# Fetching adjacency blocks in pairs, and the steps behind them one block later

## The chip, the cores and the metric

The kernel runs on one core of a Trainium2 chip. The metric is the device time of one launch in microseconds; the time shown for the kernel before is the median of three runs. The profile is of one execution, and its span runs from the first to the last instruction.

## The reference

One layer of graph attention over 4096 rows with 4 heads, then a residual and a layer norm:

```python
ht = (h @ W).reshape(N, 4, 512).transpose(1, 0, 2)
src = einsum('hnd,hd->hn', ht, a[:, :512, 0]); dst = einsum('hnd,hd->hn', ht, a[:, 512:, 0])
e = leaky_relu(src[:, :, None] + dst[:, None, :], 0.01) + adj_mat[None]
att = softmax(e, axis=-1)
h_prime = einsum('hij,hjd->hid', att, ht)
x = layernorm(x + h_prime.mean(axis=0))
```

x is 4096 x 512, adj 4096 x 4096, W 512 x 2048, a 4 x 1024 x 1, all float32. The entries of adj go up to 1e9, while the scores beside them are small. So in nearly every row of the softmax one column has all the weight: the column of the row's largest entry of adj, when it leads the second largest by enough. Then h_prime of that row is x of that column times the mean of W over heads.

## The kernel before

`leading_rows` computes every row on that assumption and counts the rows for which it can't be shown to hold (`test`, `count`, `report`); `general` computes blocks with such rows in full and runs only if there are any. With these inputs there are none, and `general` isn't entered.

The 4096 rows are cut into 32 blocks of 128, one row per partition. Row p*32 + ib belongs to block ib, so in DRAM a partition's rows of two neighbouring blocks lie side by side (adj_rows, line 99). A block of adj is 128 x 4096 float32, 2.1 MB. For each block ib:

- `segment_maxima` (VectorE, line 180, two instructions): the maximum of each segment of 16, 32 or 64 columns of adj.
- `find_segment` (lines 187 and 189, VectorE): the largest segment maximum and which segment holds it. `fetch_segment` (GpSimd, lines 196 to 207): an indirect DMA gathers that segment of each row again from DRAM, the tile lead.
- `find_column` (VectorE, lines 217 and 223, then GpSimd, lines 225 and 211): the place inside the segment, the column, and an indirect DMA that gathers the row of x for each column, the tile y.
- `turn` (PE, line 238, with a copy on ScalarE, line 240), `residual` (line 246, adds x) and `products` (line 253, y by w_sum) into one PSUM tile.
- `stats` (ScalarE, lines 275 and 277), `row_norm` (line 260), `rstd` (GpSimd, lines 280 to 282) and `finish` (line 286) make the layer norm, into the tile hold. Stores from hold are issued after the loop.

The schedule is written by hand: every engine runs its instructions in program order. The loop over t has step 1 of block t, and behind it `find_column` of block t - 2, which stands between the two halves of the reduction of block t, `turn`, `residual` and `products` of block t - 3, `stats` of block t - 4 and, every second t, `finish` of two blocks from t - 6. Through t = 14 the loop also turns and multiplies W by a on PE (`turn_w`, `head_vector`).

SP issues all plain loads and stores in order. adj has a ring of six buffers (adj_pool, AHEAD + 1); block t + 5 is issued at t, into the buffer of block t - 1, once that has been reduced. Blocks 28 to 30 are loaded in two parts and block 31 in four. x is loaded straight into hold by `load_x`: blocks 0 to 3 before the loop, 4 to 11 at t = 3, 12 to 15 at t = 11, 16 to 23 at t = 15, 28 to 31 at t = 26 and the rest at t = 31. W comes first, into the part of hold that later rows of x take. ScalarE issues the loads of a, GpSimd the gathers.

Of the kernel before, what the change touches and what calls it, by code (L numbers as in the profile page):

```python
# [9 lines left out]
F32 = mybir.dt.float32  # L10
# [60 lines left out]
def leading_rows(ctx, tc, x, adj, W, a, out, ident, v, n_bad, any_bad):  # L71
# [14 lines left out]
    PIECES = 4  # L86
    LATE = NB - Q
    BEHIND = LATE - Q

    once = ctx.enter_context(tc.tile_pool(name="once", bufs=1))  # L90
    adj_pool = ctx.enter_context(tc.tile_pool(name="adj_pool", bufs=AHEAD + 1))
    y_pool = ctx.enter_context(tc.tile_pool(name="y_pool", bufs=4))
    lead_pool = ctx.enter_context(tc.tile_pool(name="lead_pool", bufs=1))
    LEADS = (8, 8, LAST)
# [3 lines left out]

    adj_rows = adj.rearrange("(p nb) m -> nb p m", nb=NB)
    spans = ((E_EARLY, 0, EARLY), (E, EARLY, NB - LAST), (E_LAST, NB - LAST, NB))  # L100
    adj_segs = {e: adj.rearrange("n (s e) -> (n s) e", e=e) for e, _, _ in spans}
    x_rows = x.rearrange("(p nb) d -> p nb d", nb=NB)
    out_rows = out.rearrange("(p nb) d -> p nb d", nb=NB)
# [1 line left out]


    once.tile([P, 24], F32, name="pad")
    hold = once.tile([P, NB, D], F32, name="hold")
    w_at = NB - KB * H
    w_sum = once.tile([P, KB, D], F32, name="w_sum")  # L110
# [5 lines left out]
    def pieces(ib):  # L116
        return PIECES if ib == NB - 1 else 2 if ib >= LATE else 1

    def load_adj(ib):
        if 0 <= ib < NB:  # L120
            t = adj_t[ib] = adj_pool.tile([P, N], F32, name="adj_t")
            n = pieces(ib)
            for k in range(n):
                nc.sync.dma_start(t[:, ts(k, N // n)], adj_rows[ib][:, ts(k, N // n)])  # L124

    def load_x(lo, n):
        nc.sync.dma_start(hold[:, ds(lo, n), :], x_rows[:, ds(lo, n), :])
# [3 lines left out]

    load_adj(0)
    for s in range(2):
        for h in range(0, H, H // 2):
            nc.scalar.dma_start(
                a_rows[ds(s * H + h, H // 2), :], a[ds(h, H // 2), ts(s, D), :].rearrange("h d o -> h (d o)")
            )
    for kb in range(0, KB, 2):
        load_w(kb, 2)
        load_adj(kb // 2 + 1)  # L140
    for ib in range(KB // 2 + 1, AHEAD):
        load_adj(ib)
    load_x(0, Q)

    make_identity(nc, ident)
# [73 lines left out]
    def find_column(ib):  # L219
        if ib < BEHIND:  # L220
            find_inner(ib)
        within = small.tile([P, 8], U32, name="within")
        nc.vector.max_index(within, top[:, ib, :], lead_of[ib])  # L223
        col = small.tile([P, 1], U32, name="col")
        nc.gpsimd.tensor_tensor(col, at_of.pop(ib), within[:, 0:1], op=OP.add)  # L225
        gather_rows(ib, col)
# [31 lines left out]
    def row_norm(ib):  # L258
        sq = rows.tile([P, D], F32, name="sq")
        nc.scalar.activation(sq, hold[:, ib, :], AF.Square, accum_out=xx[:, ib : ib + 1])  # L260

    def put_by(ib):

        if ib == BEHIND:
            o_ps["by"] = adj_pool.tile([P, N // D, D], F32, name="adj_t")
        nc.scalar.copy(o_ps["by"][:, ib - BEHIND, :], o_ps.pop(ib))

    def add_x(engine, ib):
# [159 lines left out]
    vectors = [(kb, h) for kb in range(KB) for h in range(H)]  # L428
    vectors_at = {t: 2 if t < 3 else 1 for t in range(1, 15)}
    COLUMN, PROJECT, STATS, FINISH = 2, 3, 4, 6  # L430

    for t in range(NB):
        if t == NB // 2:
            tc.mark_branch_hint_location("general", engines=HINTED)
        if t in x_at:
            load_x(*x_at[t])
        if t + AHEAD == NB - 1:
            load_x(LATE, Q)
        load_adj(t + AHEAD)
        middle = 1 if t == NB - 1 else 2  # L440
        segment_maxima(t, 0, middle)
        if t >= COLUMN:
            find_column(t - COLUMN)
        segment_maxima(t, middle, PIECES)
        pair = FINISH <= t < BEHIND + FINISH and t % 2 == 0
        if pair:
            rstd(slice(t - FINISH, t - FINISH + 2))
        if t == NB - 1:
            for ib in (BEHIND, BEHIND + 2):
                load_x(ib, 2)  # L450
        find_segment(t)
        if t < 2:
            mean_of_heads(t)
        elif t == 2:
            mean_of_heads(2)
            mean_of_heads(3)
        if t == 0:
            turn_a()
        turned = [(*vectors[0], turn_w(*vectors.pop(0))) for _ in range(vectors_at.get(t, 0))]
        if t == 16:  # L460
            head_norms()
        ib = t - PROJECT
        if t == NB - 1:
            for late in range(LATE, NB):
                row_norm(late)
        if t == NB - 2:
            residual(LATE)
            residual(LATE + 1)
        if ib >= 0:
            turn(ib)  # L470
            if ib > BEHIND:
                products(ib - 1, KB - 1, KB)
            if ib < BEHIND:
                residual(ib)
        for some in turned:
            head_vector(*some)
        if ib >= 0:
            products(ib, 0, KB if ib < BEHIND else KB - 1)
        if t >= BEHIND + STATS:
            put_by(t - STATS)  # L480
        elif t >= STATS:
            stats(t - STATS)
            row_norm(t - STATS)
        if pair:
            finish(t - FINISH)
            finish(t - FINISH + 1)

    for ib in range(BEHIND, LATE):
        row_norm(ib)
# [217 lines left out]
```

## Time and profile before

| | |
|---|---|
| median of three runs | 235.0 us (234.98 to 235.17) |
| profiled execution | 234.9 us |
| its span | 233.4 us |
| busy: PE, VectorE, ScalarE, GpSimd | 199.9, 191.3, 111.8, 100.7 us |
| moved by DMA | 97.12 MB, of it 88.54 read from HBM and 8.39 written |
| mean DMA rate over the span | 416 GB/s |
| granted PE clock | 0.965 |

"Idle before" of an instruction is the time for which its engine had nothing to run ahead of it, and the releaser is what ended it. PE's busy time is modelled and says little on how full it is. A DMA's time to landing runs from its issue and so holds the time in which it stands behind others. In the slices each digit is a fortieth of the span in tenths.

### The profile page before, as it was taken

To read this page: it belongs to the slowest core of one execution; us is meant where nothing else is said; L and a number is where in the kernel's file an instruction comes from. 1 tells how busy PE (TensorE), PEld (TensorE's weight loads), DVE (VectorE), ACT (ScalarE), POOL (GpSimd) and SP (SyncE) were. 2 spreads that over 40 slices of the span, in tenths; PEclk is the share of its full clock that TensorE was granted. 3 is DMA by queue.
4 is the path that set the end of the run, shared out by engine and by line. 5 is a ranking of instruction groups with operands and counts; after the bars stand their busy time and mean duration, and the time that the engine had idled before them with its cause. 6 is when DMAs were issued, how large, how long until landed. Compare 5 with 4: busy or idle time off the path is not lost.

```text
span 233.4 us, 2484 instructions
## 1 busy us (share of the span) xinstructions
PE 199.9 (86%) x683; PEld 105.3 (45%) x683; DVE 191.3 (82%) x300; ACT 111.8 (48%) x267; POOL 100.7 (43%) x215
## 2 busy tenths in 40 slices
PE   0069995999999999999999779879998977999980
PEld 0034644646565555665645244334443433444460
DVE  0548299689929999999788995999999999998881
ACT  2001223014474757575767455545664644188561
POOL 2020234414524464644543452647464564548300
PEclk9999999579999999999999979999999999999997
DMA  6999999999999999999999999999999999999995
GB/s 237 423 432 428 428 438 426 415 439 436 422 421 437 423 431 425 431 419 428 430 430 428 432 423 432 423 430 421 426 433 420 426 423 426 412 424 420 421 414 213
DMA packets 12257, 97.12 MB, mean 416 GB/s; under 512 B 1992, under 2 KB 2440, under 8 KB 6480
## 3 DMA queue, kind: packets, MB, share of 16 engines
q1 hardware_dynamic: 8640, 88.08, 89.1%
q0 software_dynamic: 3584, 8.84, 9.6%
q8 instruction: 6, 0.10, 0.2%
q14 instruction: 11, 0.09, 0.1%
q10 hardware_dynamic: 16, 0.02, 0.0%
HBM read 88.54 MB, written 8.39 MB: 415 GB/s over the span
## 4 chain that ended last, share of the span: by engine, by line
DMA 64%; DVE 21%; PE 11%; SPq 1%; issue 1%; ACT 0%; DVEq 0%
DMA adj_t<-in_adj_dram 53%; DVE seg L180 17%; DMA hold<-in_x_dram 11%; PE o L253 6%; PE o L295 2%; DVE at L189 1%; PE tp L238 1%; DVE top L187 1%; PE o L246 1%; DVE within L223 1%; SPq L130 1%; PE o L291 0%; SPq L124 0%; DVE inner L217 0%; ACT hold L335 0%
## 5 line engine op out<-in xcount | busy, mean ns | idle before, releaser
L180 DVE TENSOR_REDUCE seg<-adj_t 128x128 f32<-128x2048 f32 (+3 forms) x66 | 145.5, 2208 | 28.5 <-DMA adj_t<-in_adj_dram 28.2
L253 PE MATMUL o<-w_sum,yt 128*128 128x512 f32 x248 | 117.6, 616 | 0.7 <-ACT yt L240 0.7
L253 PEld LDWEIGHTS o<-w_sum,yt 128*128 128x128 f32 x248 | 45.6, 196 | 55.2 <-issue 43.9
L240 ACT COPY yt<-tp 128x512 f32<-128x512 f32 x32 | 18.8, 588 | 43.9 <-PE tp L238 43.8
L200 POOL DMA_INDIRECT lead<-in_adj_dram,row x32 | 32.3, 1008 | 14.6 <-POOL row L196 14.6
L211 POOL DMA_INDIRECT y<-in_x_dram,col x32 | 30.9, 964 | 15.4 <-POOL col L225 15.1
L238 PE MATMUL tp<-ident,y 128*128 128x128 f32 x128 | 22.1, 296 | 10.2 <-DMA y<-in_x_dram,col 10.1
L246 PE MATMUL o<-hold,ident 128*128 128x512 f32 x52 | 28.5, 634 | 1.7 <-DMA hold<-in_x_dram 1.7
L343 PE MATMUL o<-hold,ident 128*128 128x512 f32 x32 | 17.3, 696 | 13.6 <-DMA hold<-in_L_gnn_W_dram 13.6
L238 PEld LDWEIGHTS tp<-ident,y 128*128 128x128 f32 x128 | 18.5, 209 | 22.8 <-issue 20.5
L361 ACT COPY wt<-tp 128x512 f32<-128x512 f32 x16 | 9.2, 587 | 38.2 <-PE tp L359 38.2
L196 POOL TENSOR_TENSOR row<-at,first 128x1 uint32<-128x1 uint32 x32 | 6.1, 190 | 43.6 <-DVE at L189 43.6
L367 PEld LDWEIGHTS pv<-at_d,wt 128*128 128x128 f32 x128 | 17.2, 200 | 7.4 <-ACT wt L361 3.7
L260 ACT ACTIVATE sq<-hold 128x512 f32<-128x512 f32 x32 | 19.8, 620 | 0.0
L225 POOL TENSOR_TENSOR col<-start,within 128x1 uint32<-128x1 uint32 x31 | 5.9, 190 | 32.2 <-DVE within L223 32.2
L286 ACT ACTIVATE hold<-o,nm,sd 128x512 f32<-128x512 f32 x24 | 17.2, 771 | 0.0
L277 ACT ACTIVATE sq<-o,nm 128x512 f32<-128x512 f32 x24 | 16.5, 687 | 0.8
L343 PEld LDWEIGHTS o<-hold,ident 128*128 128x128 f32 x32 | 6.9, 225 | 21.5 <-issue 21.5
L367 PE MATMUL pv<-at_d,wt 128*128 128x2 f32 x128 | 16.0, 249 | 0.6 <-ACT wt L361 0.6
L344 ACT ACTIVATE w_sum<-o 128x512 f32<-128x512 f32 x4 | 2.4, 598 | 27.5 <-PE o L343 27.5
L275 ACT ACTIVATE sq<-o 128x512 f32<-128x512 f32 x24 | 14.5, 606 | 0.0
L187 DVE MAX8 top<-seg 128x8 f32<-128x256 f32 (+2 forms) x32 | 11.6, 362 | 1.1
(86 smaller groups left out, 140.0 us busy)
## 6 DMA issues: line engine op xcount, KB each, us to landing
adj_t<-in_adj_dram SPq DMA_DIRECT2D x28, 2048.0 KB, 30.8
adj_t<-in_adj_dram SPq DMA_DIRECT2D x6, 1024.0 KB, 28.1
hold<-in_L_gnn_W_dram SPq DMA_DIRECT2D x2, 2048.0 KB, 16.4
hold<-in_x_dram SPq DMA_DIRECT2D x2, 2048.0 KB, 37.6
out_dram<-hold SPq DMA_DIRECT2D x4, 1024.0 KB, 16.1
out_dram<-hold SPq DMA_DIRECT2D x7, 512.0 KB, 14.4
hold<-in_x_dram SPq DMA_DIRECT2D x3, 1024.0 KB
adj_t<-in_adj_dram SPq DMA_DIRECT2D x4, 512.0 KB, 19.8
```

The lines of the kernel that those rows point to most:

```text
L180: nc.vector.tensor_reduce(seg_of[ib][:, ts(k, N // e // n)], adj_t[ib][:, ts(k, N // n)].rearrange("p (s e) -> p s e", e=e), axis=AX.X, op ...
L200: nc.gpsimd.indirect_dma_start(out=lead, out_offset=None, in_=adj_segs[e], in_offset=bass.IndirectOffsetOnAxis(ap=row[:, :1], axis=0),)
L211: nc.gpsimd.indirect_dma_start(out=y, out_offset=None, in_=x, in_offset=bass.IndirectOffsetOnAxis(ap=col[:, :1], axis=0),)
L238: nc.tensor.transpose(tp[:, kb, :], y[:, ds(kb, P, KB)], ident)
L240: nc.scalar.copy(yt, tp)
L246: nc.tensor.matmul(o_ps[ib], ident, hold[:, ib, :], start=start, stop=False)
L253: nc.tensor.matmul(o_ps[ib], yt_of[ib][:, kb, :], w_sum[:, kb, :], start=(start and kb == 0), stop=(kb == KB - 1),)
L260: nc.scalar.activation(sq, hold[:, ib, :], AF.Square, accum_out=xx[:, ib : ib + 1])
L277: nc.scalar.activation(sq, o, AF.Square, bias=nm[:, i], accum_out=sd[:, i])
L286: nc.scalar.activation(hold[:, ib, :], o_ps.pop(ib), AF.Identity, bias=nm[:, i], scale=sd[:, i])
L343: nc.tensor.matmul(o, ident, hold[:, w_at + kb * H + h, :], start=(h == 0), stop=(h == H - 1))
L367: nc.tensor.matmul(pv[:, kb, h : 2 * H : H], wt[:, k, :], at_d[:, k, h : 2 * H : H], start=(k == 0), stop=(k == KB - 1),)
```

## The change

The pool of six adj buffers becomes one tile, ring, with six slots; block ib is in slot ib % 6. A new function `load_pair` fetches two blocks with one transfer into two neighbouring slots. The blocks named by PAIRED (4 to 15) are for the pair branch of the loop, which issues at every even t. From t = 5 to t = 18 (SLACK) what stands behind `find_segment` runs one block later than before (`steps` holds t - 1 instead of t; at t = 5 it is empty, at t = 19 it holds 18 and 19). The rows of a are loaded by two transfers instead of four. `put_by` takes the same slot of the ring as before. Reductions, index searches, gathers and products themselves are unchanged.

```diff
--- before.py
+++ after.py
@@ -86,9 +86,10 @@
     PIECES = 4
     LATE = NB - Q
     BEHIND = LATE - Q
+    SLOTS = AHEAD + 1
+    PAIRED = range(4, 16)
 
     once = ctx.enter_context(tc.tile_pool(name="once", bufs=1))
-    adj_pool = ctx.enter_context(tc.tile_pool(name="adj_pool", bufs=AHEAD + 1))
     y_pool = ctx.enter_context(tc.tile_pool(name="y_pool", bufs=4))
     lead_pool = ctx.enter_context(tc.tile_pool(name="lead_pool", bufs=1))
     LEADS = (8, 8, LAST)
@@ -98,6 +99,7 @@
 
     adj_rows = adj.rearrange("(p nb) m -> nb p m", nb=NB)
     spans = ((E_EARLY, 0, EARLY), (E, EARLY, NB - LAST), (E_LAST, NB - LAST, NB))
+    adj_pairs = adj.rearrange("(p nb) m -> p nb m", nb=NB)
     adj_segs = {e: adj.rearrange("n (s e) -> (n s) e", e=e) for e, _, _ in spans}
     x_rows = x.rearrange("(p nb) d -> p nb d", nb=NB)
     out_rows = out.rearrange("(p nb) d -> p nb d", nb=NB)
@@ -105,6 +107,7 @@
 
 
     once.tile([P, 24], F32, name="pad")
+    ring = once.tile([P, SLOTS, N], F32, name="adj_t")
     hold = once.tile([P, NB, D], F32, name="hold")
     w_at = NB - KB * H
     w_sum = once.tile([P, KB, D], F32, name="w_sum")
@@ -116,9 +119,15 @@
     def pieces(ib):
         return PIECES if ib == NB - 1 else 2 if ib >= LATE else 1
 
+    def load_pair(ib):
+        slot = ib % SLOTS
+        for k in range(2):
+            adj_t[ib + k] = ring[:, slot + k, :]
+        nc.sync.dma_start(ring[:, ds(slot, 2), :], adj_pairs[:, ds(ib, 2), :])
+
     def load_adj(ib):
         if 0 <= ib < NB:
-            t = adj_t[ib] = adj_pool.tile([P, N], F32, name="adj_t")
+            t = adj_t[ib] = ring[:, ib % SLOTS, :]
             n = pieces(ib)
             for k in range(n):
                 nc.sync.dma_start(t[:, ts(k, N // n)], adj_rows[ib][:, ts(k, N // n)])
@@ -131,15 +140,13 @@
 
     load_adj(0)
     for s in range(2):
-        for h in range(0, H, H // 2):
-            nc.scalar.dma_start(
-                a_rows[ds(s * H + h, H // 2), :], a[ds(h, H // 2), ts(s, D), :].rearrange("h d o -> h (d o)")
-            )
+        nc.scalar.dma_start(a_rows[ts(s, H), :], a[:, ts(s, D), :].rearrange("h d o -> h (d o)"))
     for kb in range(0, KB, 2):
         load_w(kb, 2)
         load_adj(kb // 2 + 1)
-    for ib in range(KB // 2 + 1, AHEAD):
+    for ib in range(KB // 2 + 1, PAIRED[0]):
         load_adj(ib)
+    load_pair(PAIRED[0])
     load_x(0, Q)
 
     make_identity(nc, ident)
@@ -262,7 +269,7 @@
     def put_by(ib):
 
         if ib == BEHIND:
-            o_ps["by"] = adj_pool.tile([P, N // D, D], F32, name="adj_t")
+            o_ps["by"] = ring[:, (ib + 2) % SLOTS, :].rearrange("p (b d) -> p b d", d=D)
         nc.scalar.copy(o_ps["by"][:, ib - BEHIND, :], o_ps.pop(ib))
 
     def add_x(engine, ib):
@@ -428,23 +435,34 @@
     vectors = [(kb, h) for kb in range(KB) for h in range(H)]
     vectors_at = {t: 2 if t < 3 else 1 for t in range(1, 15)}
     COLUMN, PROJECT, STATS, FINISH = 2, 3, 4, 6
+    SLACK = range(5, PAIRED[-1] + 4)
 
     for t in range(NB):
+        steps = [t - 1] if t in SLACK else [t]
+        if t == SLACK[0]:
+            steps = []
+        elif t == SLACK[-1] + 1:
+            steps = [t - 1, t]
         if t == NB // 2:
             tc.mark_branch_hint_location("general", engines=HINTED)
         if t in x_at:
             load_x(*x_at[t])
         if t + AHEAD == NB - 1:
             load_x(LATE, Q)
-        load_adj(t + AHEAD)
+        if t + AHEAD in PAIRED[2:]:
+            if t % 2 == 0:
+                load_pair(t + AHEAD - 1)
+        else:
+            load_adj(t + AHEAD)
         middle = 1 if t == NB - 1 else 2
         segment_maxima(t, 0, middle)
-        if t >= COLUMN:
-            find_column(t - COLUMN)
+        for u in steps:
+            if u >= COLUMN:
+                find_column(u - COLUMN)
         segment_maxima(t, middle, PIECES)
-        pair = FINISH <= t < BEHIND + FINISH and t % 2 == 0
-        if pair:
-            rstd(slice(t - FINISH, t - FINISH + 2))
+        pairs = [u - FINISH for u in steps if FINISH <= u < BEHIND + FINISH and u % 2 == 0]
+        for ib in pairs:
+            rstd(slice(ib, ib + 2))
         if t == NB - 1:
             for ib in (BEHIND, BEHIND + 2):
                 load_x(ib, 2)
@@ -459,31 +477,35 @@
         turned = [(*vectors[0], turn_w(*vectors.pop(0))) for _ in range(vectors_at.get(t, 0))]
         if t == 16:
             head_norms()
-        ib = t - PROJECT
         if t == NB - 1:
             for late in range(LATE, NB):
                 row_norm(late)
         if t == NB - 2:
             residual(LATE)
             residual(LATE + 1)
-        if ib >= 0:
-            turn(ib)
-            if ib > BEHIND:
-                products(ib - 1, KB - 1, KB)
-            if ib < BEHIND:
-                residual(ib)
+        for u in steps:
+            ib = u - PROJECT
+            if ib >= 0:
+                turn(ib)
+                if ib > BEHIND:
+                    products(ib - 1, KB - 1, KB)
+                if ib < BEHIND:
+                    residual(ib)
+            for some in turned:
+                head_vector(*some)
+            turned = []
+            if ib >= 0:
+                products(ib, 0, KB if ib < BEHIND else KB - 1)
+            if u >= BEHIND + STATS:
+                put_by(u - STATS)
+            elif u >= STATS:
+                stats(u - STATS)
+                row_norm(u - STATS)
         for some in turned:
             head_vector(*some)
-        if ib >= 0:
-            products(ib, 0, KB if ib < BEHIND else KB - 1)
-        if t >= BEHIND + STATS:
-            put_by(t - STATS)
-        elif t >= STATS:
-            stats(t - STATS)
-            row_norm(t - STATS)
-        if pair:
-            finish(t - FINISH)
-            finish(t - FINISH + 1)
+        for ib in pairs:
+            finish(ib)
+            finish(ib + 1)
 
     for ib in range(BEHIND, LATE):
         row_norm(ib)
```

## The prediction

> **What bounds the kernel now.** I read the page first: the slices and the DMA queues (parts 2 and 3). Columns of the queue lines are packets, MB and share of sixteen engines' span.
>
> ```profile
> DVE  0548299689929999999788995999999999998881
> DMA  6999999999999999999999999999999999999995
> GB/s 237 423 432 428 428 438 426 415 439 436 422 421 437 423 431 425 431 419 428 430 430 428 432 423 432 423 430 421 426 433 420 426 423 426 412 424 420 421 414 213
> ...
> q1 hardware_dynamic: 8640, 88.08, 89.1%
> q0 software_dynamic: 3584, 8.84, 9.6%
> ```
>
> The DMA engines are full from the second slice to the last but one, at 412 to 439 GB/s whatever the stage does: 89.1 + 9.6 = 98.7% of the span is packets. Time is bytes, unless something else falls behind. The chain of waits agrees:
>
> ```profile
> DMA 64%; DVE 21%; PE 11%; SPq 1%; issue 1%; ACT 0%; DVEq 0%
> ```
>
> VectorE is the only other candidate, so its timeline is the second view; start, duration and, in brackets, idle time before with its cause:
>
> ```profile
> 18.34 4.48 DVE L180 TENSOR_REDUCE seg<-adj_t 128x128 f32<-128x2048 f32 x2 [4.20 <-DMA adj_t<-in_adj_dram]
> ...
> 28.07 2.29 DVE L180 TENSOR_REDUCE seg<-adj_t 128x128 f32<-128x2048 f32 x1 [4.25 <-DMA adj_t<-in_adj_dram]
> ...
> 47.62 2.29 DVE L180 TENSOR_REDUCE seg<-adj_t 128x128 f32<-128x2048 f32 x1 [2.67 <-DMA adj_t<-in_adj_dram]
> ...
> 69.15 2.29 DVE L180 TENSOR_REDUCE seg<-adj_t 128x128 f32<-128x2048 f32 x1 [4.03 <-DMA adj_t<-in_adj_dram]
> ```
>
> ```profile
> 115.83 2.29 DVE L180 TENSOR_REDUCE seg<-adj_t 128x128 f32<-128x2048 f32 x1 [1.29 <-DMA adj_t<-in_adj_dram]
> ...
> 142.66 2.29 DVE L180 TENSOR_REDUCE seg<-adj_t 128x64 f32<-128x2048 f32 x1 [2.37 <-DMA adj_t<-in_adj_dram]
> ```
>
> These are the reductions of blocks 1, 2, 5, 8, 16 and 20, each starting as its block lands. Prices follow. Blocks 1 and 2 are two 2.1 MB transfers apart: 9.73 / 2 = 4.87 us per 2.1 MB, which I call a unit. The indirect gathers cost 9.6% of 233.4 us over 32 blocks, 0.70 us per block. Check: from block 5 to block 8 SP's queue carries adj 6, adj 7, x 4 to 11 (one unit) and adj 8, so 4 x 4.87 + 3 x 0.70 = 21.6; measured 69.15 - 47.62 = 21.5. From 8 to 16: 8.5 x 4.87 + 8 x 0.70 = 47.0; measured 46.7. An adj-only block therefore arrives every 5.6 us, and VectorE takes 5.66 us for one in the first 18 blocks (starts at 69.15, 74.83, 80.49) and about 5.4 later. Both run neck and neck; of 28.2 us that VectorE waits for adj, 23.8 lie at or before block 8 (8.67, 4.20, 4.25, 2.67, 4.03), only 4.4 after it.
>
> **What the Trainium skill says.** All four from "DMA: Bandwidth & Descriptors". "Issuing engines are not separate DMA queues": transfers of SP, ACT and GpSimd share the same sixteen engines; the trace agrees, since q1 and q0 add up to the whole span. "Where 436 GB/s comes from": the fabric ceiling is 435 GB/s; 2.097 MB in 4.87 us is 431, so 1% is left. "Queues, rings and completion order": an engine alternates between rings a packet at a time; the trace fits, as a lead gather lands 6.1 us after issue beside 16 KB packets and 5.3 beside 8 KB ones (issues at 177 to 189 us). "Two DMAs through the same engine are not ordered": a transfer over bytes that an earlier one writes must wait for its semaphore; no run shows it yet, the change makes such a case.
>
> **The change part by part.**
>
> *A block too many.* PAIRED is 4 to 15. The prologue fetches 0 to 3 and the pair (4, 5). In the loop only t + 5 in 6 to 15 goes to the pair branch; at t = 0, t + 5 = 5 is not, and falls to load_adj(5), which fetches block 5 a second time. SP's order confirms it: 17 whole-block transfers and 6 pairs are 29 blocks where there were 28 (blocks 28 to 31 go in parts in both). That adds 2.097 MB: 4.87 us by the unit, 4.95 by the queue's mean (208.0 us for 88.08 MB). I take 4.9. With the engines at 98.7% no idle time covers it.
>
> *Its wait.* The second fetch overwrites a half that the pair writes, so SP waits for the pair's landing. Behind it in SP's order stand pairs 6-7 and 8-9 and x 4 to 11; VectorE waits for these. The queue's cover is x 0 to 3, half a unit, 2.4 us. The first transfer took 7.69 us from issue to landing, 2.8 over its unit, so at worst the engines stand 0.4 us; part of the 2.8 is not start-up, and a gather falls there. I take 0, keep 0.4.
>
> *Pairs.* Six transfers of 4.2 MB for twelve of 2.1. Bytes are the same. Rows of a pair join, so packets may grow from 16 to 32 KB; the trace's packet records show 611 ns for 16 KB and 309 for 8 KB, some 7 ns each beside the bytes. Eight packets per engine per pair, six pairs: 48 x 7 ns = 0.34 us, an estimate. Bounds: 0 if packets stay 16 KB; at best the fabric's ceiling over 12 units, 58.4 us x 1.1% = 0.6. I take 0.2.
>
> *What comes late.* A pair lands as a whole, so its first block waits for its second. Worked forward from block 2 (28.07) with the prices above:
> - VectorE is through block 3 at 39.3, as before. Pair 4-5 is 3 units and 2 row gathers later: 28.07 + 14.6 + 1.4 = 44.1. Idle 4.8. Block 4 ends 49.7.
> - Second block 5: half a unit of x, one unit, one gather: 52.1. Idle 2.4. Block 5 has no steps behind it (5.4 us): ends 57.5.
> - Pair 6-7: two units, no row gather: 61.9. Idle 4.4. Two blocks: 73.2.
> - x 4 to 11 and pair 8-9: 3 units and two gathers: 77.9. Idle 4.7.
>
> Block 8 starts at 77.9, not 69.15: 8.8 us late. Pairs 10-11, 12-13 and 14-15 then land at 89.0, 100.2 and 111.3, and VectorE wants them at 89.2, 100.5 and 111.9: no wait. Each is issued when its slots' second block is reduced (57, 73 and 89), 22 to 32 us ahead, so the engines stay fed. VectorE works on without a gap: block 16 at 77.9 + 8 x 5.66 = 123.2; then 7.9 with the head norms (2.25, from 121.5 to 123.75 before), 5.7, 5.4 and 5.7 (block 19 has two steps) give block 20 at 147.9. DMA has it at 142.66 + 4.9 = 147.6. Late by 0.3, VectorE makes it up at 0.2 per block, 5.4 against 5.6. So the 8.8 melts to DMA's 4.9: the x loads, in which VectorE used to wait, are the cover. Without it the cost would be 8.8.
>
> *The steps one block later.* No instruction is added; inner, within (0.17 each, 0.07 load), the row gather, transposes, residual, products, stats and finish move. A lead gather has one block more: before, issue 75.71, use 82.68, 7.0 us for a landing of 6.1; now 12.6. If 32 KB packets added what 8 to 16 KB added twice over (1.6), 7.7 would still fit. Without the shift this would stall VectorE up to 0.7 per block. PE gets rows later; its turns ran 6.11 us apart up to 112 us, short of its own time, but later it takes 4.95 (117.83, 122.81, 127.73) against 5.6 per block, and waits for rows. Block 19's double step is 5 us of PE work, made up at 0.65 per block by about block 27. ACT is at 48%, POOL at 43%. Cost 0; if not made up, up to 1.
>
> *Rows of a.* Two ACT transfers for four, 0.0% of DMA time: 0. It also takes waits off SP's adj 2 and 3, but the queue is four units deep there.
>
> Sum on the profiled execution: 234.9 + 4.9 - 0.2 = 239.6, of which the span is 233.4 + 4.7 = 238.1 and 1.5 lies around it. The median shown is 0.1 higher: 239.7.
>
> **Rivals.**
> 1. *VectorE becomes the bound.* Slack after block 8 is 4.4, lateness 8.8; that alone gives +4.4, under DMA's 4.9, so 0.5 us more lateness is free, and anything beyond lasts. It needs pairs landing late (the queue dry at the second block 5), a lead gather over 12.6 us, or PE not caught up at block 31. For it: three near ties above. Against: the x loads give room again. One to three us more: 240.5 to 243.
> 2. *Pairs move faster than bytes allow here.* If longer rows lift the read rate, the gain is on 12 blocks. Up to the ceiling it is 0.6 (239.2). To end not slower it must win 4.9 us, 0.41 on each 4.87, so that a pair's unit takes 4.46 or less, 470 GB/s: above every slice and the skill's ceiling. From that point on the forecast turns: 235 or less. Also on that side, but excluded by the order of SP, is that the second fetch isn't there.
> 3. *The second fetch starves the engines.* If SP's wait and start-up aren't covered by x, add 0.4 to 2.8: 240.1 to 242.5, with a notch in the DMA slice near 45 us.
>
> **How the numbers follow.** Forecast 0.74 (239.3 to 240.1); rival 1 0.12; rival 3 0.08; rival 2 within the ceiling or a little over 0.03, to 235 or less 0.03. The range 239.0 to 241.5 takes the forecast whole and the nearer half of rivals 1 and 3. A difference of 0.2% (0.5 us) can be told from none. Faster 0.02, same 0.01, slower 0.97.
>
> **What would show it.** HBM read up by 2.1 MB to 90.6; q1's share near 89%, DMA slices all 9; adj groups of 17 and 6 transfers, 4.2 MB the latter. VectorE idle before blocks 4, 5, 6 and 8 of 4.8, 2.4, 4.4 and 4.7 us, none from 8 to 19, and block 20 starting near 148. The last quarter of block 31 near 211.9 (207.19 before). Wrong if block 20 starts after 150, if VectorE waits for leads, or if a unit between landings is clearly under 4.8 us.

## The result: slower, by far more than forecast

The kernel after takes 255.9 us (median of four, 255.1 to 256.9) against 235.1: a ratio of 1.089, 95% interval 1.085 to 1.093. The forecast was 239.7 with a range to 241.5. The direction was right, the size was not: 20.8 us are lost, not 4.7. The profiled execution took 256.9 us with a span of 255.3, 21.9 over the span before. Times here and below are medians of the fast runs; in four kernels (block 5 once, the moved steps alone, the norms in two, the light W) one or two runs lie over 1.5% above the fastest and are left out.

The page of the kernel after, slices, queues and the shares of the chain:

```profile
DVE  0636693673957999799950999767939999989782
DMA  6999999999999999999999999999999999972134
GB/s 259 431 431 433 435 435 410 446 432 403 447 442 429 413 424 434 414 426 432 420 431 432 429 427 429 421 440 421 417 426 424 418 423 420 424 301 87 42 151 184
...
q1 hardware_dynamic: 7920, 90.18, 83.2%
...
DMA 38%; PE 34%; issue 10%; POOL 9%; ACT 4%; DVE 3%; POOLq 0%; ACTq 0%; DVEq 0%
```

The extra 2.1 MB are there (90.18 MB for 88.08), and the DMA engines still run full through slice 35. But then they run dry: the last four slices are at 2, 1, 3 and 4 tenths where they were at 9, 9, 9 and 5. The last quarter of adj is issued at 198.6 and lands some 11 us later, about 45 us before the end; VectorE takes it only behind 227.3. The rest of the kernel hasn't kept up. Of the chain that ended last, DMA has 38%, where it had 64%. The bound has passed from bytes to what waits on the computing engines and on the gathers. VectorE's timeline says when; start, duration and, in brackets, the idle time before and its cause:

```profile
43.31 2.29 DVE L187 TENSOR_REDUCE seg<-adj_t 128x128 f32<-128x2048 f32 x1 [4.13 <-DMA adj_t<-in_adj_dram]
...
77.93 2.29 DVE L187 TENSOR_REDUCE seg<-adj_t 128x128 f32<-128x2048 f32 x1 [3.80 <-DMA adj_t<-in_adj_dram]
...
104.15 0.18 DVE L224 MAX8 inner<-lead 128x8 f32<-128x16 f32 x1 [1.30 <-DMA lead<-in_adj_dram,row]
...
139.18 0.19 DVE L386 TENSOR_REDUCE n<-px 128x8 f32<-128x32 f32 x1 [7.96 <-PE px L384]
...
168.28 0.20 DVE L224 MAX8 inner<-lead 128x8 f32<-128x32 f32 x1 [3.64 <-DMA lead<-in_adj_dram,row]
175.04 0.20 DVE L224 MAX8 inner<-lead 128x8 f32<-128x32 f32 x1 [1.30 <-DMA lead<-in_adj_dram,row]
189.79 0.20 DVE L224 MAX8 inner<-lead 128x8 f32<-128x32 f32 x1 [3.94 <-DMA lead<-in_adj_dram,row]
...
227.09 0.09 DVE L230 MATCH_VALUE_LOAD within<-top,lead 128x8 f32 x1 [1.12 <-DMA lead<-in_adj_dram,row]
```

Block 8 starts at 77.93 where 77.9 was worked out. Blocks 4, 5 and 6 on the way there miss by 0.7 or 0.8 us, one early and two late, and the misses cancel. After block 8 VectorE never waits for adj again, so its 4.4 us of later adj waits are gone, and new waits have come. The sum closes nearly: block 8 is 8.8 late, less 4.4 is 4.4; waits for leads come to 1.30 + 0.35 + 3.64 + 1.30 + 3.94 + 1.12 = 11.6 where they were 0.2, adding 11.4; the wait for the head norms went from 1.1 to 8.0, adding 6.9. Together 22.7. The last line, the search that stands in the reduction of block 31, began at 204.23 before and begins at 227.09 now: 22.9. The tail behind it is 1.0 shorter (28.2 for 29.2), which leaves the 21.9 of the span.

Who is late for VectorE shows in the table of waits (engine and line that waits, what it waits for; us in total, times, longest). The kernel after:

```profile
POOL sd L287 <- ACT sq L284: 33.0, 8, 6.5
PE tp L245 <- DMA y<-in_x_dram,col: 21.9, 9, 6.7
DVE inner L224 <- DMA lead<-in_adj_dram,row: 10.5, 5, 3.9
DVE n L386 <- PE px L384: 8.0, 1, 8.0
PE o L253 <- ACT hold L293: 3.4, 1, 3.4
```

The kernel before:

```profile
POOL sd L280 <- ACT sq L277: 8.0, 5, 3.3
PE tp L238 <- DMA y<-in_x_dram,col: 10.1, 10, 2.7
DVE n L379 <- PE px L377: 1.1, 1, 1.1
```

PE waits twice as long for gathered rows, and GpSimd four times as long for ScalarE's statistics. The second matters for VectorE, because GpSimd works in order and `rstd` stands ahead of the block's own segment gather. GpSimd's timeline after:

```profile
182.60 0.19 POOL L287 TENSOR_SCALAR sd<-sd 128x2 f32<-128x2 f32 x1 [5.37 <-ACT sq L284]
...
184.30 1.06 POOL L207 DMA_INDIRECT lead<-in_adj_dram,row  x1 [0.28 <-POOL row L203]
```

GpSimd stands for 5.37 us at `rstd`, and the gather of block 22's lead goes out behind it, 6 us after its segment was found (178.3). It lands 5.5 us later, and VectorE, which wants it two blocks on, waits 3.94 us for it (189.79 above). So there is a ring: late rows make PE late, PE the statistics, these the gather of a lead, and the gather VectorE. Lateness of PE, which I had counted as harmless, has a way to VectorE. The head norms, which VectorE wants from PE at t = 16, are a second way.

Not every wait for a lead is this ring. The wait of 1.30 at 175.04 is (4.92 us at `rstd`, at 166.57). Those of 1.30 at 104.15 and of 0.35 behind it are for gathers that took 12.6 and 14.4 us to land. That of 3.64 is for one that took 9.3, issued behind the two row gathers of the double step at t = 19.

### The profile page after: what moved, and what is told of

Same layout as the page of the kernel before. It is cut to its first block, busy times and chain, and to the rows that moved or that the text cites. A ratio compares the mean times of both kernels' runs of the same rounds, so it can differ in the third digit from the quotient of the medians.

```text
span 255.3 us, 2465 instructions
## 1 busy us (share of the span) xinstructions
PE 206.2 (81%) x683; PEld 109.2 (43%) x683; DVE 190.7 (75%) x300; ACT 112.1 (44%) x267; POOL 100.2 (39%) x215
## 3 DMA queue, kind: packets, MB, share of 16 engines
q1 hardware_dynamic: 7920, 90.18, 83.2%
HBM read 90.64 MB, written 8.39 MB: 388 GB/s over the span
## 4 chain that ended last, share of the span: by engine, by line
DMA 38%; PE 34%; issue 10%; POOL 9%; ACT 4%; DVE 3%; POOLq 0%; ACTq 0%; DVEq 0%
PE o L260 21%; DMA adj_t<-in_adj_dram 19%; DMA y<-in_x_dram,col 18%; PE o L253 5%; PE tp L245 4%; POOL lead L207 3%; POOL y L218 2%; DVE seg L187 2%; PE pv L374 2%; POOL sd L288 1%; PE o L302 1%; DMA a_rows<-in_L_gnn_a_dram 1%; ACT sq L284 1%; ACT sq L282 1%; ACT yt L247 1%
## 5 line engine op out<-in xcount | busy, mean ns | idle before, releaser
L260 PE MATMUL o<-w_sum,yt 128*128 128x512 f32 x248 | 121.0, 631 | 0.8 <-ACT yt L247 0.7
L260 PEld LDWEIGHTS o<-w_sum,yt 128*128 128x128 f32 x248 | 47.2, 202 | 58.7 <-issue 47.1
L245 PE MATMUL tp<-ident,y 128*128 128x128 f32 x128 | 22.1, 297 | 21.9 <-DMA y<-in_x_dram,col 21.9
L253 PE MATMUL o<-hold,ident 128*128 128x512 f32 x52 | 30.3, 671 | 5.9 <-ACT hold L293 3.4
L245 PEld LDWEIGHTS tp<-ident,y 128*128 128x128 f32 x128 | 19.5, 207 | 33.2 <-issue 32.3
L350 PE MATMUL o<-hold,ident 128*128 128x512 f32 x32 | 17.7, 711 | 13.4 <-DMA hold<-in_L_gnn_W_dram 13.4
L374 PEld LDWEIGHTS pv<-at_d,wt 128*128 128x128 f32 x128 | 18.0, 209 | 8.4 <-issue 4.4
L374 PE MATMUL pv<-at_d,wt 128*128 128x2 f32 x128 | 16.9, 256 | 1.3 <-ACT wt L368 1.3
L287 POOL TENSOR_SCALAR sd<-sd 128x2 f32<-128x2 f32 (+1 forms) x13 | 2.5, 191 | 33.4 <-ACT sq L284 33.0
## 6 DMA issues: line engine op xcount, KB each, us to landing
adj_t<-in_adj_dram SPq DMA_DIRECT2D x6, 1024.0 KB, 12.5
```

The source lines that it names most:

```text
L245: nc.tensor.transpose(tp[:, kb, :], y[:, ds(kb, P, KB)], ident)
L253: nc.tensor.matmul(o_ps[ib], ident, hold[:, ib, :], start=start, stop=False)
L260: nc.tensor.matmul(o_ps[ib], yt_of[ib][:, kb, :], w_sum[:, kb, :], start=(start and kb == 0), stop=(kb == KB - 1),)
L350: nc.tensor.matmul(o, ident, hold[:, w_at + kb * H + h, :], start=(h == 0), stop=(h == H - 1))
L374: nc.tensor.matmul(pv[:, kb, h : 2 * H : H], wt[:, k, :], at_d[:, k, h : 2 * H : H], start=(k == 0), stop=(k == KB - 1),)
```

## The experiments

Each kernel ran on the chip beside the kernel before, whose median was 235.0 to 235.1 each time. Ratios are of means and can differ a little from the quotient of the medians. Letters in an expectation are theories of that round. First round: P holds the pairs' joined packets, which make gathers late, to be the cause; S the moved steps; L adj itself, which comes late. Second round: Q holds the two crossings into VectorE's way (the statistics and the norms) to be enough to carry the loss; R that it comes whatever is uncrossed, by gathers late of themselves or by way of the buffers of y. Then T holds PE to be a second bound, with no room to make up for lost time while it works on W, and G the gathers to set the pace; U holds the work on W in PE to be what makes it late, V the late gathers and the double step. The two last runs use S and L anew and say for what. All diffs are against the kernel after and show its main lines; "..." marks what is left out.

### Parts alone and parts undone

**Block 5 fetched once.**

```diff
-        else:
+        elif t + AHEAD not in PAIRED:
             load_adj(t + AHEAD)
```

> The changed kernel without the second fetch of block 5; pairs and late steps stay. Theory P (the pairs' 32 KB packets make the gathers late, PE loses time that it can't make up while it still turns W, then statistics, the rstd on GpSimd and the gathers queued behind it follow): about 251, the 4.9 us of the bytes and no more, gathers still land 10 to 16 us after issue. Theory S (the steps one block later put PE's and GpSimd's work too late for head_norms at t = 16 and the double step at t = 19): about 251 too. Theory L (what is late is adj itself: the pair as a whole and the second block 5, 8.8 us at block 8): about 240, since half of that lateness goes.

Measured: 251.0 us, ratio 1.073 (1.066 to 1.079), 4.9 less than the change in full. That is the price forecast, known to some two us, since the runs of this kernel spread from 249.4 to 251.2. L, with its 240, falls. But the price isn't paid as the forecast said, through a full DMA queue, since the engines are idle at the end in both: block 8 starts at 73.12 instead of 77.93, 4.8 earlier, and VectorE carries that through.

**The moved steps alone**, with adj as before.

```diff
-    for ib in range(KB // 2 + 1, PAIRED[0]):
+    for ib in range(KB // 2 + 1, AHEAD):
         load_adj(ib)
-    load_pair(PAIRED[0])
...
-        if t + AHEAD in PAIRED[2:]:
-            if t % 2 == 0:
-                load_pair(t + AHEAD - 1)
-        else:
-            load_adj(t + AHEAD)
+        load_adj(t + AHEAD)
```

> The kernel before with the steps of t = 5 to 18 one block later and a in two transfers; adj in single transfers, each block once. P: 235, within 0.5, gathers 6 and 8 us. S: 248 to 252, with VectorE waiting for PE at head_norms and for leads about t = 20. L: 235.

Measured: 240.5 us, ratio 1.020 (1.017 to 1.024). None of the theories: not free, and not the bulk. VectorE's waits in it:

```profile
125.98 0.19 DVE L385 TENSOR_REDUCE n<-px 128x8 f32<-128x32 f32 x1 [5.11 <-PE px L383]
...
154.34 0.20 DVE L223 MAX8 inner<-lead 128x8 f32<-128x32 f32 x1 [2.89 <-DMA lead<-in_adj_dram,row]
161.94 0.20 DVE L223 MAX8 inner<-lead 128x8 f32<-128x32 f32 x1 [2.15 <-DMA lead<-in_adj_dram,row]
174.39 0.20 DVE L223 MAX8 inner<-lead 128x8 f32<-128x32 f32 x1 [1.65 <-DMA lead<-in_adj_dram,row]
```

Head norms and, after the double step at t = 19, leads: the same two ways as in the change in full, with no pair in the kernel.

**Packets of 16 KB**: slots of the ring stand 32 bytes apart, so that a pair's two rows no longer join.

```diff
-    ring = once.tile([P, SLOTS, N], F32, name="adj_t")
+    ring = once.tile([P, SLOTS, N + 8], F32, name="adj_t")
...
-        nc.sync.dma_start(ring[:, ds(slot, 2), :], adj_pairs[:, ds(ib, 2), :])
+        nc.sync.dma_start(ring[:, ds(slot, 2), :N], adj_pairs[:, ds(ib, 2), :])
```

> The changed kernel with 32 bytes between the slots of the ring, so that a pair's rows don't join and its packets are 16 KB; transfers, their order, the second fetch and the late steps are the same. P: about 240, the forecast without the packets' gain, and gathers land after 6 to 9 us throughout. S and L: 255 to 256 as the changed kernel.

Measured: 252.4 us, ratio 1.074 (1.071 to 1.077), 3.5 less; P wanted 240, S and L 255. GpSimd's wait for statistics falls from 33.0 to 18.0 us, the head norms' from 8.0 to 2.8. But the gap has a price of its own: 16 KB packets take 625 ns on average where they took 615 in the kernel after. So 3.5 is what is left after that loss.

**The steps in time**, pairs and second fetch kept.

```diff
-        steps = [t - 1] if t in SLACK else [t]
-        if t == SLACK[0]:
-            steps = []
-        elif t == SLACK[-1] + 1:
-            steps = [t - 1, t]
+        steps = [t]
```

> The changed kernel with every step at its old block; pairs of 32 KB packets and the second fetch stay. P: 256 or more, for a lead gather of 10 to 14 us no longer fits into the 7 us it has and stalls VectorE in most of blocks 6 to 17. S: about 240. L: 255.

Measured: 248.6 us, ratio 1.058 (1.056 to 1.060), 7.3 less. No theory had this: P wanted 256 or more, S 240, L 255. The wait for statistics is back at 5.4 us and the head norms' at 1.4. In exchange VectorE waits for leads while pairs fly:

```profile
88.69 0.18 DVE L224 MAX8 inner<-lead 128x8 f32<-128x16 f32 x1 [1.71 <-DMA lead<-in_adj_dram,row]
...
98.06 0.18 DVE L224 MAX8 inner<-lead 128x8 f32<-128x16 f32 x1 [3.61 <-DMA lead<-in_adj_dram,row]
...
105.97 0.18 DVE L224 MAX8 inner<-lead 128x8 f32<-128x16 f32 x1 [2.16 <-DMA lead<-in_adj_dram,row]
```

So the extra block does cover leads. Where its 7.3 us are lost shows when blocks are set side by side. First block 20 and the search in the reduction of block 31 in the kernel with steps in time, then block 20 in the kernel after, whose search is the line at 227.09 above.

```profile
157.34 2.27 DVE L187 TENSOR_REDUCE seg<-adj_t 128x64 f32<-128x2048 f32 x1
...
218.73 0.09 DVE L230 MATCH_VALUE_LOAD within<-top,lead 128x8 f32 x1 [0.93 <-DMA lead<-in_adj_dram,row]
```

```profile
157.02 2.27 DVE L187 TENSOR_REDUCE seg<-adj_t 128x64 f32<-128x2048 f32 x1
```

Up to block 20 the two are level: with the moved steps VectorE waits 6.2 us less for leads (1.7 for 7.9) and 6.5 more for the head norms (8.0 for 1.4). The whole difference comes behind block 20, after the double step at t = 19, in waits for leads of 3.64, 1.30 and 3.94 where this kernel has 0.31.

### Undoing the crossings

**`rstd` behind the block's own segment gather** on GpSimd.

```diff
-        for ib in pairs:
-            rstd(slice(ib, ib + 2))
...
         find_segment(t)
+        for ib in pairs:
+            rstd(slice(ib, ib + 2))
```

> The changed kernel with the rstd of a pair behind the block's own segment gather in GpSimd's order instead of ahead of it. Theory Q (VectorE loses 11.6 us waiting for leads because GpSimd stands up to 6.5 us at rstd for ScalarE's statistics, and the segment gather is queued behind it; and 6.9 us more at head_norms, where the norms' matmul is queued behind products on a late PE): 244 to 248, the lead waits nearly gone and the wait at head_norms still there. Rival R (the gathers are late of themselves, or PE's lateness comes back through the y buffers, so what stands ahead of them is no matter): 254 to 256.

Measured: 252.5 us, ratio 1.073 (1.067 to 1.079), between Q's 248 and R's 254. VectorE's waits for leads fall from 11.6 to 8.1 us, so the ring through `rstd` is a part of them.

**VectorE's part of the head norms at t = 22** instead of 16.

```diff
         if t == 16:
-            head_norms()
+            norms = head_norms()
+        if t == 22:
+            bound_of_heads(norms)
...
```

> The changed kernel with head_norms in two parts: the matmul stays at t = 16, VectorE's and ScalarE's work on its result goes to t = 22. Q: 248 to 251, the 8 us wait for PE at t = 16 gone and the lead waits still there. R: the 8 us come back as other waits, 254 to 256.

Measured: 254.1 us, ratio 1.078 (1.076 to 1.081), as R had it.

**Both**, and **both with block 5 fetched once.**

> The changed kernel with both edits, rstd behind the segment gather and head_norms in two parts. Q: 239.5 to 241.5, that is 235 and the 4.9 us of the second fetch with at most 1.5 over, VectorE meeting adj again by about block 22. R: over 250.

> The changed kernel with both edits and without the second fetch of block 5. Q: 235 to 236.5, nothing left of the change but the forecast's small terms. R: over 246.

Measured: 254.3 us, ratio 1.082 (1.080 to 1.084), and 248.0 us, ratio 1.056 (1.053 to 1.059). Q falls: two edits that win 3.4 and 1.8 us alone win 1.6 together. The waits of the kernel with both show why:

```profile
POOL sd L287 <- ACT sq L284: 23.9, 7, 5.8
...
DVE both L392 <- ACT n L390: 9.5, 1, 9.5
```

The wait for the norms has moved, no smaller, to the next instruction in which VectorE needs ScalarE, and ScalarE is behind PE. With these two ways uncrossed, the late engine meets VectorE at the next one. The way through the buffers of y, which R names, is small: in the kernel after, GpSimd's waits for PE come to 2.8 us in all.

### How late PE is, and what that costs

**W's vectors early**: the nine of t = 6 to 14 are done at t = 6, 7 and 8, three each, ahead of the turn. First in the change in full, then in the moved steps alone, then with block 5 fetched once and 16 KB packets (gap of 32 bytes).

```diff
-    vectors_at = {t: 2 if t < 3 else 1 for t in range(1, 15)}
+    vectors_at = {t: 2 if t < 3 else 1 for t in range(1, 6)}
+    more_at = {6: 3, 7: 3, 8: 3}
...
+        for _ in range(more_at.get(t, 0)):
+            head_vector(*vectors[0], turn_w(*vectors.pop(0)))
```

> The changed kernel with the nine W vectors of t = 6 to 14 at t = 6, 7 and 8, three each, ahead of the block's turn. Theory T (PE is the second bound: with one W vector per block it needs 6.11 us where adj comes every 5.6, so what it loses by idling before t = 9, and at half clock after that, stays lost up to t = 14 and reaches VectorE by ScalarE's statistics, GpSimd's rstd and head_norms): 243 to 248, no wait for PE at head_norms and under 4 us of waits for leads. Rival G (GpSimd and the slow gathers beside 32 KB packets set the pace, PE only waits for them): 254 to 256.

> The kernel before with the steps of t = 5 to 18 one block later and a in two transfers, single transfers of adj, and the W vectors at t = 6, 7 and 8. T: 235 to 237, against 240.8 with one vector per block. G: 240 to 241.5.

> The changed kernel without the second fetch, with 16 KB packets and with the W vectors at t = 6, 7 and 8; pairs and late steps stay. T: 235 to 237.5. G and a theory in which the late steps cost by the double step at t = 19 alone: 240 to 243.

Measured: 260.7, 255.1 and 261.5 us, ratios 1.108 (1.105 to 1.111), 1.088 (1.082 to 1.094) and 1.115 (1.108 to 1.123). The first is 4.8 us slower than the change in full, the second 14.6 slower than the moved steps alone, and the third slower than the change in full too, where T had hoped for gains. The edit is bad in itself: a vector alone takes some 2.2 us, each product waiting 0.7 for its copy on ScalarE. So it doesn't test T. But it serves as a dose. PE's turn of block 4, in the moved steps alone and then in the second of these kernels:

```profile
71.18 0.64 PE L244 MATMUL tp<-ident,y 128*128 128x128 f32 x4
```

```profile
96.74 1.09 PE L244 MATMUL tp<-ident,y 128*128 128x128 f32 x4
```

Waits and VectorE's timeline of the second:

```profile
POOL sd L286 <- ACT sq L283: 50.7, 9, 21.1
```

```profile
107.78 0.18 DVE L223 MAX8 inner<-lead 128x8 f32<-128x16 f32 x1 [14.01 <-DMA lead<-in_adj_dram,row]
```

25.6 us of lateness put into PE come out as 21.1 at `rstd`, as 14.0 at VectorE's lead, and as 14.6 in the time. That is the ring of the first section, driven hard: some of PE's lateness is taken up on the way, and what reaches VectorE stays in the time.

**A light W**: from the fifth vector on, three quarters of W's transposes and products are left out (the norms, and so the test on them, mean nothing then). In the change in full and in the moved steps alone.

```diff
-        for k in range(KB):
+        n = 1 if kb * H + h > 3 else KB
+        for k in range(n):
             nc.tensor.transpose(tp[:, k, :], hold[:, w_at + kb * H + h, ts(k, P)], ident)
...
```

> The changed kernel with three quarters of the W vectors' PE work left out from the fifth vector on (one of four transposes and one of four products each; the bound that guards the answer is then of no meaning, and the rows are computed in full). Theory U (PE's work through t = 14 has no slack, 6.11 us a block against adj's 5.6; what it loses there reaches VectorE through the waits on ScalarE, GpSimd and the norms): 242 to 247, VectorE not waiting for PE at the norms. Rival V (PE's lateness only follows from late gathers and from the double step at t = 19): 253 to 256.

> The kernel before with the steps of t = 5 to 18 one block later, a in two transfers and the same three quarters of the W vectors' work left out. U: 235 to 237.5, from 240.8 with them. V: 239.5 to 241, with the waits for leads after t = 19 as large as before.

Measured: 253.5 us, ratio 1.082 (1.080 to 1.085), and 239.0 us, ratio 1.017 (1.016 to 1.019): 2.4 and 1.5 us less. U falls. In the first, the head norms' wait halves (3.9 for 8.0), but PE then waits longer for rows (30.4 us in all, where it was 21.9). W's work is a small part of what makes PE late. In the second, the head norms' wait is gone (0.6), and what is left of the loss sits behind the double step: PE waits 3.4 us for ScalarE's `finish` and VectorE then 4.2 for a lead.

### Pairs alone

Pairs, block 5 once, steps in time, 16 KB packets with the gap of 32 bytes; then the same with x 0 to 3 ahead of the first pair on SP; then that order with the moved steps and the light W.

```diff
     load_pair(PAIRED[0])
-    load_x(0, Q)
...
+    load_x(0, Q)
     load_pair(PAIRED[0])
```

> The kernel before with the blocks 4 to 15 in pairs of 16 KB packets, each block once, steps in time, a in two transfers. If lateness of a pair as a whole costs nothing for itself: 235 to 235.5. T: 236 to 239, since rows come to PE 5 us late at blocks 4 to 8 and PE can't make that up before t = 14. G: 235 to 236.

> Blocks 4 to 15 in pairs of 16 KB packets, each once, steps in time, as in the run that gave 239.1, but x 0 to 3 issued ahead of the first pair instead of behind it. U: 235 to 236.5, since PE no longer stands 6.5 us for x at its first residual and starts block 1's turn near 51 as in the kernel before. V, or any theory by which the pairs cost through adj's own lateness: 238.5 to 240.

> The changed kernel with block 5 fetched once, 16 KB packets, x 0 to 3 ahead of the first pair and the light W vectors; pairs and late steps stay. U: 235 to 238. V: 241 or more.

Measured: 239.1 us, ratio 1.017 (1.016 to 1.019); 239.3 us, ratio 1.021 (1.016 to 1.025); 244.0 us, ratio 1.037 (1.035 to 1.039). In the first, PE waits 6.5 us for x, which stands behind a pair in SP's order; the second takes that wait away and gains nothing. I had blamed x, wrongly: in both the DMA engines are full to the end, at packets of 625 ns. How much of the loss is the gap, the next runs show. In the third, the moved steps, with the light W, cost 4.7 us over the second, in line with the runs above.

Two runs compare packets without the gap of 32 bytes: the pairs of the change as they are, block 5 once and steps in time, and the same with slots 512 bytes apart.

```diff
-    ring = once.tile([P, SLOTS, N], F32, name="adj_t")
+    ring = once.tile([P, SLOTS, N + 128], F32, name="adj_t")
```

> Pairs as in the changed kernel, joined to packets of 32 KB; block 5 fetched once; steps not moved. Computes all. Theory S (joined packets cost by themselves: gathers land after 10 us and more and VectorE waits for leads in the pair phase, as it did for 7.5 us with steps in time and a second fetch): 242 to 245, DMA no longer full at the end. Theory L (joined packets cost only beside lateness that the second fetch and the moved steps make): 235.5 to 238, lead waits under 2.

> The same, but slots of the ring 512 bytes apart, so that packets stay 16 KB without the gap of 32 bytes that the other runs with 16 KB had. Computes all. If the gap of 32 bytes slowed these runs' transfers: packets back at 611 to 614 ns mean, 235 to 236.5. If it was the pair itself: packets at 618 to 624 ns and 239, as with the gap of 32 bytes. S: less than the other run by 6 or more; L: within 2 of it.

Measured: 243.0 us, ratio 1.034 (1.032 to 1.036), and 238.0 us, ratio 1.013 (1.011 to 1.015). With the wide gap, packets are back at a mean of 614 ns and a median of 611, as in the kernel before. But the time falls by 1.1 us only, from 239.1, where 235 to 236.5 was expected: the gap of 32 bytes was the smaller part of that loss. The two runs differ in how rows join: 5.0 us between them is the price of joined packets, as S had it, if a little less. VectorE in the kernel with joined ones, while pairs fly:

```profile
83.59 0.18 DVE L224 MAX8 inner<-lead 128x8 f32<-128x16 f32 x1 [1.95 <-DMA lead<-in_adj_dram,row]
...
91.92 0.18 DVE L224 MAX8 inner<-lead 128x8 f32<-128x16 f32 x1 [2.58 <-DMA lead<-in_adj_dram,row]
...
99.86 0.18 DVE L224 MAX8 inner<-lead 128x8 f32<-128x16 f32 x1 [2.19 <-DMA lead<-in_adj_dram,row]
```

And how long a lead's gather takes from issue to landing, for gathers issued between 44 and 112 us, joined packets first, then 16 KB ones:

```profile
DMA to landing us min/median/max: 6.2/9.0/13.0
```

```profile
DMA to landing us min/median/max: 6.0/6.3/8.3
```

A 32 KB packet holds an engine for 1213 ns (median of 768 records) where a 16 KB one holds it for 611. The Trainium skill, "DMA: Bandwidth & Descriptors", "Queues, rings and completion order", says that an engine switches between rings only at the end of a packet. A gather's packets then have longer ones to wait for. The trace fits this and shows the size: a gather takes some half as much again, on the median (9.0 for 6.3) and at the worst (13.0 for 8.3).

### The loss, laid out

Five kernels make a staircase, each with one part more:

| kernel | us | step | what the step is |
|---|---|---|---|
| before | 235.1 | | |
| pairs, 16 KB packets (wide gap) | 238.0 | 2.9 | a pair lands as a whole; block 8 starts 5.0 later |
| pairs, joined packets | 243.0 | 5.0 | gathers land late |
| and block 5 twice | 248.6 | 5.6 | block 8 starts 5.4 later still |
| and steps one block later (after) | 255.9 | 7.3 | PE late behind the double step, and through it GpSimd and VectorE |

The first step isn't the late block 8 alone, which would leave 5.0 less the 4.4 of later adj waits, 0.6. In that kernel VectorE also waits longer for leads (2.4 us for 0.2) and for the head norms (2.4 for 1.1).

Another order divides a little differently: the second fetch is worth 4.9 with the steps moved; the moved steps cost 5.5 without pairs and 8.0 with pairs and block 5 once (251.0 for 243.0). In both of these, too, all or nearly all of the loss lies behind the double step. With block 5 once, block 20 starts at 152.03 with the moved steps and at 152.09 without, and the search in block 31's reduction at 220.47 and 213.75. Without pairs, moved steps start block 20 at 143.82 for 142.66 and that search at 211.59 for 204.23. The rows of a in two transfers and the ring as one tile were in all of these kernels but not tried alone. No kernel here beats the one before, nor could fetching in pairs be expected to: 98.7% of its span is packets.

## Why the prediction was wrong

**"A block too many" and "Its wait" were right.** 4.9 to 5.6 us for a forecast of 4.9; HBM read 90.64 MB; the DMA slices show no notch near 45 us, so rival 3 is out. The reason given, that DMA has no idle time to cover it, no longer applied: in the kernel after, the cost comes through the late blocks on VectorE.

**"Pairs" was right in what it counted** and missed what mattered. Packets did grow to 32 KB, at 1213 ns for twice 611: 9 ns for each, 0.4 us in all. What the same packets do to the gathers beside them stood under another step.

**"What comes late" was right to block 8, and then overtaken.** Idle times before blocks 4, 5, 6 and 8 are 4.1, 3.8, 4.3 and 3.8 (forecast 4.8, 2.4, 4.4 and 4.7); that block 8 is exact is partly luck, since these misses cancel. Block 16 starts at 125.06 for 123.2. Block 20 starts at 157.02 for 147.9. Seven of those nine us are the head norms. With steps in time it starts at 157.34, held up by leads instead, so the nine are owed to late gathers, whichever way they reach VectorE. One premise was also thin: DMA and VectorE in a near tie, with 4.4 us of slack left against 8.8 of lateness, so that each later us of VectorE's counts in full.

**"The steps one block later" is the step that failed**: cost 0, at most 1, and measured 7.3 in the changed kernel. Four of its sentences broke.

- "Block 19's double step is 5 us of PE work, made up at 0.65 per block by about block 27." This is the sentence that carries the 7.3, all of which lies behind that step. PE had no arrears when it came, for it waits 3.23 us for a row at 152.42, just ahead of it. Then PE stands 3.35 us for `finish`, since the four PSUM tiles of its sums are all taken, and the two matmuls behind that take 2.08 us instead of 1.02. The statistics come late, GpSimd waits 4.92 and 5.37 us for them at `rstd`, and VectorE waits for the leads gathered behind it. It isn't made up: at block 24 VectorE still waits 3.94 us.

```profile
152.42 0.73 PE L245 MATMUL tp<-ident,y 128*128 128x128 f32 x4 [3.23 <-DMA y<-in_x_dram,col]
...
167.80 2.08 PE L253 MATMUL o<-hold,ident 128*128 128x512 f32 x2 [3.35 <-ACT hold L293]
```

- "If 32 KB packets added what 8 to 16 KB added twice over (1.6), 7.7 would still fit." They added up to 8: leads landed in 11.0 us on the median and 14.4 at most while pairs flew, rows y in 12.5 and 16.6 at most (8.1 and 9.2 before). And only the lead's gather was given a block more. `find_column` and `turn` moved together, so y has no more cover than before. The prediction costed the first gather and not the second, whose lateness goes straight to PE. So the shift didn't hide the 5.0 us of the joined packets: what it saved at leads came back at the head norms.
- PE "waits for rows", as if that were room. A PE that waits doesn't stay at its price. PE's timeline, and its busy time, granted clock (fourth column) and DMA share in a stretch after such a wait:

```profile
77.13 1.10 PE L245 MATMUL tp<-ident,y 128*128 128x128 f32 x4 [6.66 <-DMA y<-in_x_dram,col]
```

```profile
42.50:48.00 5.50, 2.67 (x6) 0.50 1.04 429
```

The Trainium skill, "TensorE: Matmul & The Clock Gate", "Part 1: The HAM clock gate", has the array at half clock after an idle window of some 3.4 us. The trace agrees: 0.50 after 4.8 us without work, and four transposes in 1.10 us instead of 0.65. The turn at 77.13, with its wait of 6.66, has the next one 9.8 us behind it, where turns ran 6.11 apart.
- "ACT is at 48%, POOL at 43%." The working took busy shares for room and didn't follow the order of each engine. In order, `rstd` stands ahead of the segment gather, and a late statistic holds the gather back. Share says nothing on that; the line with 33.0 us does.

The other terms that the forecast of 239.7 missed are smaller: 5.2 on the packets (a gain of 0.2 forecast, a loss of 5.0 measured), 2.9 on the pair that lands as a whole (0 forecast) and 0.7 on the second fetch. With the 7.3 that makes 16.1 of the 16.2 between forecast and result.

**Of the rivals, the first was right in kind and not in size.** "VectorE becomes the bound" through late leads and a PE not caught up is what happened. It had a chance of 0.12 and one to three us; it took some 16 on top of the second fetch's 4.9. It was sized from VectorE's slack, with no path for lateness to come back. The list of what would make the prediction wrong named it: block 20 after 150, and VectorE waiting for leads.

**What stays open.** That the double step carries the 7.3 is read from the traces of three pairs of kernels with and without moved steps; no run moved the steps without one. What the late rows and the empty step at t = 5 would cost if leads were not late beside them isn't settled. That the half clock adds to PE's lateness is read from traces too, and no run took it away.

## What to carry to other kernels

An engine's busy share is no room to be late in: before moving a step, follow each engine's order to the next instruction that another engine waits for, and see what is queued behind it. A stretch of delayed steps ends in a block that holds two, and here that block, and not the stretch, cost the time. A large transfer is priced by the small gathers that share its engines, too, and not by its own bytes alone: look at issue to landing of the smallest transfers beside it. And where one engine is full and a second in a near tie with it, work out what happens to each us by which the second falls behind, since nothing gives it back.

## What the runs showed of the hardware

- Joining rows to 32 KB packets leaves the time per byte nearly as it was (9 ns saved on 1222) and lengthens an indirect gather beside them from 6.3 to 9.0 us on the median, and from 8.3 to 13.0 at most.
- With slots 16 KB + 32 bytes apart in SBUF, 16 KB packets average 625 ns; they average 614 without the gap and 614 with one of 512 bytes. The gap also moves the tiles behind the ring, and 8 KB packets slow with it (317 ns for 310), so it needn't be the slots alone. With pairs alone that was 1.1 us of the time (239.1 against 238.0), which I first put down to the order of x.
